# Two decoder layers on one Trainium2 core: the opening's norms and fills re-ordered, and three small loads moved to another queue

## The chip, the cores and the metric

The kernel runs as one program on one core of a Trainium2 chip. Its engines work side by side, each through its own queue in the queue's order: TensorE (PE, with its weight loads shown as PEld), VectorE (DVE), ScalarE (ACT), GpSimd (POOL) and SyncE (SP, which here only issues transfers). ACT and POOL issue transfers too. An engine waits for another by a semaphore, and what stands behind a waiting instruction in the same queue waits with it. The metric is device microseconds (us) of one execution; the figure of a kernel is the median of several.

## The reference

The input is a batch of B = 2 sequences of 1024 tokens with 128 channels, float32 throughout. Two layers follow one another; each adds an attention and then a feed-forward to `x`, each on a layer norm of `x`:

```python
x = x + _L0_attn_ref(_layernorm(x, axis=-1), Wq, bq, Wk, bk, Wv, bv, proj)   # causal, 16 heads of 64
x = x + _L0_ffn_ref(_layernorm(x, axis=-1), W, Wp, bp, sim, temp, Wd0, Wu0, ...) # low-rank experts, top 1 of 4
x = x + _L1_attn_ref(_layernorm(x, axis=-1), W_k, W_v, W_o)                  # 16 heads of 8, scores by distance
x = x + _L1_ffn_ref(_layernorm(x, axis=-1), Wr1, br1, Wr2, br2, Ws1, ...)    # 8 experts, top 2, and a shared one
```

with

```python
def _layernorm(x, axis=-1, eps=1e-05):
    m = jnp.mean(x, axis=axis, keepdims=True)
    v = jnp.var(x, axis=axis, keepdims=True)
    return (x - m) / jnp.sqrt(v + eps)
```

Only the opening of the first layer is touched by the change: the first layer norm, the transposition of its result and of the weights, and some constants.

## The kernel before

The 2048 tokens are 16 tiles of 128 (tokens on the partitions, channels along the row), and lie in `x` as [128, 16, 128]. For loads, norms and the first projections four tiles go together as a group of 512 tokens; groups 0 and 1 are the first sequence, 2 and 3 the second. Four transfers on SP's queue (L80) bring them in this order.

The opening, up to about 41 us, has these steps:

- Loads of the attention's weights `nat_q`, `nat_k`, `nat_v` as [128, 8, 128] (L259): the first of eight chunks of each on ACT's queue, then the biases `bnat`, then the other seven chunks on ACT and SP. After them come the weights of later parts: `proj`, `raw_*` on SP, and `vnat`, `wr`, `br`, `raw_be`, `be` on POOL. The last three on SP's queue are `simI`, `bp` and `temp` (L298, L300, L302), small inputs of the expert choice.
- `layernorm_T(b)` (L117 to L135) for the two groups of a sequence: `bn_stats` and `bn_aggr` for four tiles (L123, L124), then the reciprocal root by `rsqrt`: a bound on VectorE (L99), a logarithm and an exponential on ScalarE (L102, L103), and one refining step of four small VectorE operations (L106 to L109, each 128x4). Then four `tensor_scalar` make the normalized tiles `xn` (L130; three buffers are there for them), TensorE transposes each (L134), and one VectorE copy of 128x512 brings the four from PSUM to `xnT` (L135).
- `turn_nat` transposes chunks of the weights on TensorE, four to a PSUM bank, and VectorE copies them to `wqkvT`: the first chunk of all three together (L327), the other 21 chunks in six copies (L325). The banks of kind `tr`, into which all these transposes go, are four.
- `project(units[0])` makes the queries, keys and values of the first pair of heads of the first sequence, from groups 0 and 1. For q and k a half of the group's product (64 output rows, 512 columns) is one matmul on half of the array; ScalarE takes q (L421) and v (L437) out of PSUM, VectorE k (L429). The banks of kind `acc` are four.
- `small_weights()` transposes and combines the other parts' weights, with a path that goes back and forth between TensorE, VectorE, ScalarE and, for the mask of `bd`, POOL (L388, L392). It reads `simI`, `bp` and `temp`.
- `sides_of_rows()` makes `side_of`, four columns that the second layer's attention uses: a memset of `row` (128x512) and six small ones (L332, L337), a product with the identity (L339), all on POOL, and a sum on VectorE (L340).
- `fill(own[0], G)` presets two column ranges of a buffer of the second layer's attention: 128x2816 and 128x128 elements, strided, on POOL (L171, L172).

In this part a scheduler orders each engine's queue. It decides from its own estimates which ready instruction goes next, so an engine's order is not the order of the source: before, the statistics of all four groups stand ahead of the first refining step on VectorE, and POOL's work for `row` and `own` stands behind its loads.

From the first scores (`scp`, L69) on, the queues of PE, DVE, ACT and POOL are written out by hand (`manual_schedule`), item by item: scores of a tile pair, softmax, transposes (`flipp`, L501), the product with v (`zp`), and in the gaps the projections of the next heads and the feed-forward. It is the larger part of the time; the change leaves its orders as they are.

Of the kernel before, what the change touches and what calls it, by code (L numbers as in the profile page):

```python
# [9 lines left out]
FP = mybir.dt.float32  # L10
AF = mybir.ActivationFunctionType
ALU = mybir.AluOpType
AX = mybir.AxisListType

P = 128
EPS = 1e-5
# [4 lines left out]
def two_layers(ctx: ExitStack, tc: tile.TileContext, a: dict, out: bass.AP):  # L21
    nc = tc.nc
    V, S, G, T = nc.vector, nc.scalar, nc.gpsimd, nc.tensor

    B, SEQ, D = a["L0_attn_x"].shape
# [5 lines left out]
    NG = TOK // 512  # L31
# [3 lines left out]
    NP = a["L0_ffn_Wp"].shape[0]  # L35
    H1, DK = 16, 8
# [7 lines left out]
    small = ctx.enter_context(tc.tile_pool(name="small", bufs=4))  # L44
# [10 lines left out]
    def bank(tag):  # L55
        n, size = banks["tags"][tag]
        return banks["pool"].tile([P, size, 512], FP, tag=tag, name=f"{tag}p", bufs=n)
# [4 lines left out]
    def tr():  # L62
        return bank("tr").rearrange("p o (j q) -> p (o j) q", q=P)
# [7 lines left out]
    def bcast(ap, axis, shape):  # L71
        return ap.unsqueeze(axis).to_broadcast(list(shape))
# [11 lines left out]
    ident = const.tile([P, P], FP, name="ident")  # L84
# [10 lines left out]
    def rsqrt_parts(y, v, least, op):  # L95
        c = small.tile(list(v.shape), FP, tag="rsq", name="rsq")

        def bound():
            V.tensor_scalar(c, v, least, None, op)  # L99

        def guess():
            S.activation(y, c, AF.Ln)  # L102
            S.activation(y, y, AF.Exp, scale=-0.5)  # L103

        def refine():
            V.tensor_tensor(c, c, y, ALU.mult)  # L106
            V.tensor_tensor(c, c, y, ALU.mult)
            V.tensor_scalar(c, c, -0.5, 1.5, ALU.mult, ALU.add)  # L108
            V.tensor_tensor(y, y, c, ALU.mult)  # L109

        return bound, guess, refine

    def rsqrt(*of):
        for part in rsqrt_parts(*of):
            part()


    def layernorm_T(b):
        for g in range(b * NG // B, (b + 1) * NG // B):
            mv = small.tile([P, 4, 2], FP, tag="mv", name="mv")  # L120
            for j in range(4):
                st = small.tile([P, V.BN_STATS_DIM], FP, tag="st", name="st")
                V.bn_stats(st, x[:, 4 * g + j, :])  # L123
                V.bn_aggr(mv[:, j, :], st)  # L124
            rstd = small.tile([P, 4], FP, tag="rstd", name="rstd")
            rsqrt(rstd, mv[:, :, 1], EPS, ALU.add)
            t = tr()
            for j in range(4):
                xn = work.tile([P, D], FP, tag="xn", name="xn")
                V.tensor_scalar(  # L130
                    xn, x[:, 4 * g + j, :], mv[:, j, 0:1], rstd[:, j : j + 1],
                    ALU.subtract, ALU.mult,
                )
                T.transpose(t[:, j, :], xn, ident)  # L134
            V.tensor_copy(xnT[:, bass.ts(g, 512)], t.rearrange("p j q -> p (j q)"))  # L135

    def transposed(dst, src):

        n, m = src.shape
        t = tr()  # L140
        T.transpose(t[:m, 0, :n], src, ident[:n, :n])
        V.tensor_copy(dst, t[:m, 0, :n])
# [19 lines left out]
    side_of = const.tile([P, 4], FP, name="side_of")  # L162
    pre = ExitStack()
    pp0 = pre.enter_context(tc.tile_pool(name="pre", bufs=1, side="right"))
    own = [pp0.tile([P, NB, H1, 32], FP, name="own0")]
# [4 lines left out]
    def fill(side, eng):  # L170
        eng.memset(flat(side, slice(DK + 2, 32)), 0.0)  # L171
        eng.memset(flat(side, slice(DK + 2, DK + 3)), 1.0)  # L172
# [55 lines left out]
    with ExitStack() as l0:  # L228
# [22 lines left out]
        stage = early.enter_context(tc.tile_pool(name="stage", bufs=1))  # L251
# [5 lines left out]
        def load_nat(eng, i, cs):  # L257
            w = a[f"L0_attn_W{'qkv'[i]}"].rearrange("h d e -> (h d) e").rearrange("(c p) e -> p c e", p=P)
            eng.dma_start(nat[i][:, cs, :], w[:, cs, :])  # L259

        for i in range(3):
            load_nat(nc.scalar, i, slice(0, 1))
        bnat = stage.tile([2 * NC, P], FP, name="bnat")
        for i, k in enumerate("qk"):
            nc.scalar.dma_start(
# [4 lines left out]
        load_nat(nc.scalar, 0, slice(1, NC))  # L270
        load_nat(nc.sync, 1, slice(1, NC))
        load_nat(nc.scalar, 2, slice(1, NC))
        vnat = stage.tile([H, 2, DH], FP, name="vnat")
        for r in range(2):
            nc.gpsimd.dma_start(vnat[:, r, :], a["L0_attn_bv"])
# [14 lines left out]
        for i in range(4):  # L290
            r = slice(roff[i], roff[i] + ranks[i])
            nc.sync.dma_start(raw["wd"][r, :], a[f"L0_ffn_Wd{i}"])
            for j in range(2):
                nc.sync.dma_start(
                    raw["wu"][:, j * DH + r.start : j * DH + r.stop], a[f"L0_ffn_Wu{i}"]
                )
        simI = stage.tile([NP, 4 + NP], FP, name="simI")
        nc.sync.dma_start(simI[:, :4], a["L0_ffn_sim"])  # L298
        bp = stage.tile([NP, 1], FP, name="bp")
        nc.sync.dma_start(bp, a["L0_ffn_bp"].unsqueeze(1))  # L300
        temp = stage.tile([P, 1], FP, name="temp")
        nc.sync.dma_start(temp, a["L0_ffn_temp"].partition_broadcast(P))  # L302
        nc.gpsimd.dma_start(wr1, a["L1_ffn_Wr1"])
        nc.gpsimd.dma_start(br1, a["L1_ffn_br1"].unsqueeze(1))
        nc.gpsimd.dma_start(wr2, a["L1_ffn_Wr2"])
# [6 lines left out]
        xnT = xnp.tile([P, TOK], FP, tag="xnT", name="xnT")  # L312
        xn2T = xnp.tile([P, TOK], FP, tag="xnT", name="xn2T")

        def turn_nat(*which):

            t, at = tr(), 0
            for i, cs in which:
                for c in cs:
                    T.transpose(t[:, at, :], nat[i][:, c, :], ident)  # L320
                    at += 1
            i, cs = which[0]
            if len(which) == 1:
                dst = wqkvT[:, i, cs[0] * P : (cs[-1] + 1) * P]
                V.tensor_copy(dst, t[:, :at, :].rearrange("p j q -> p (j q)"))  # L325
            else:
                V.tensor_copy(wqkvT[:, :, cs[0] * P : (cs[0] + 1) * P], t[:, :at, :])  # L327

        def sides_of_rows():

            row = stage.tile([P, 4, 4, 32], FP, name="row")
            G.memset(row, 0.0)  # L332
            for k, part, value in (
                (0, slice(0, DK), 1.0), (0, slice(DK + 1, DK + 2), 1.0), (1, slice(DK, DK + 1), 1.0),
                (2, slice(0, DK), 2.0), (2, slice(DK, DK + 1), 1.0), (3, slice(DK + 1, DK + 2), 1.0),
            ):
                G.memset(row[:, k, :, part], value)  # L337
            row = row.rearrange("p k h j -> p k (h j)")
            G.tensor_tensor(row, row, bcast(ident, 1, [P, 4, P]), ALU.mult)  # L339
            V.tensor_reduce(side_of, row, AX.X, ALU.add)  # L340

        def small_weights():
            sc, dn, pr = D + NR, D, D + NR + 4
# [159 lines left out]
        def keep(it, hh):  # L503
            i = it["i"]
            copy = (V.tensor_copy, S.copy)[hh]
            copy(  # L506
                it["group"]["pT", hh][:, : i + 1, i % 2].rearrange("p j r u -> p r j u"), it["t", hh]
            )
# [238 lines left out]
                    items.append(units[n + 1]["items"][i])  # L747
        items += [units[-1]["items"][i] for i in (2, 3, 0, 1)]
        tail = items.index(units[-2]["items"][4])
        turn_nat(*[(i, [0]) for i in range(3)])  # L750
        transposed(bqk, bnat)

        V.tensor_scalar(bqk[:, :NC], bqk[:, :NC], -SC, None, ALU.mult)
        layernorm_T(0)
        for piece in project(units[0]):
            piece()
        layernorm_T(1)
        for i in range(3):
            for cs in (range(1, 5), range(5, NC)):
                turn_nat((i, cs))  # L760
        transposed(bz, vnat.rearrange("h r d -> h (r d)"))
        V.tensor_scalar(bz, bz, SC, None, ALU.mult)
        small_weights()
        sides_of_rows()
        early.close()
        pp = l0.enter_context(tc.tile_pool(name="pp", bufs=3))
        tp = l0.enter_context(tc.tile_pool(name="tp", bufs=1))
# [5 lines left out]
            mybir.EngineType.PE, mybir.EngineType.DVE, mybir.EngineType.Activation, mybir.EngineType.Pool  # L773
        }
        l0.enter_context(tc.manual_schedule(engines=order))
        fill(own[0], G)
        n = 0
        events = {}
        turns = []
# [595 lines left out]
    with ExitStack() as f1:  # L1375
# [4 lines left out]
        xnT = xnT1[0]  # L1380
# [160 lines left out]
```

## Time and profile before

| what | value |
|---|---|
| median of 3 runs | 1081.24 us (1080.89, 1081.24, 1086.43) |
| profiled execution | 1079.92 us |
| its span, first to last instruction | 1078.2 us |
| granted TensorE clock, mean | 0.978 |
| busy: PE, ACT, DVE, POOL | 94%, 63%, 56%, 32% of the span |
| share of the chain that ended last | PE 80%, DVE 10%, ACT 6% |
| first scores of the first layer's attention | 40.99 us after the start |

A row of the timeline gives the start in us, the duration in us of the run of like instructions that it merges, the engine, the line of the kernel, the operation, what it writes and reads, and in brackets how long the engine had been idle and what ended that. A row of the chain of work that ended last gives the start, the time that the step takes on the chain, and engine, output and line. In the table of stretches the columns are the stretch, its length, the busy time and number of instructions of PE, PEld, DVE, ACT and POOL, the granted clock, the share of the DMA engines and GB/s.

### The profile page before, as it was taken

How to read it: one execution, taken by the hardware profiler on the slowest of the kernel's cores; microseconds unless marked ns; L12 is line 12 of the kernel's file. 1: busy time of each engine (PE TensorE's matmuls, PEld its weight loads, DVE VectorE, ACT ScalarE, POOL GpSimd, SP SyncE). 2: the span in 40 equal slices, each digit the busy share in tenths (PEclk: the TensorE clock that was granted, in tenths of full speed). 3: DMA queues.
4: the chain of work that ended last, by engine and by line, in shares of the span. 5: the costliest groups of instructions: out<-in, count | busy, mean ns of one | idle time of the engine just before them, and what ended most of it. 6: DMA issues, size and time to landing. Idle time of an engine off the chain costs nothing.

```text
span 1078.2 us, 26161 instructions
## 1 busy us (share of the span) xinstructions
PE 1009.4 (94%) x10662; PEld 610.0 (57%) x10662; DVE 599.8 (56%) x1770; ACT 680.9 (63%) x1294; POOL 340.4 (32%) x480
## 2 busy tenths in 40 slices
PE   4899999999999999999788989999999999789998
PEld 1466767666666666666566323323333332679986
DVE  6676676787878878686675323301433310365652
ACT  1376666666666666666465767788776788534541
POOL 4133344343534444434353110000001221023764
PEclk9899999999999999999999999999999999888999
DMA  5000000000000000000001400000000100011222
GB/s 131 1 2 2 2 2 2 2 2 2 2 2 2 2 3 2 1 2 2 2 2 61 117 1 2 2 1 1 20 2 6 30 18 16 10 30 46 79 79 57
DMA packets 27574, 20.13 MB, mean 19 GB/s; under 512 B 3699, under 2 KB 25054, under 8 KB 27454
## 3 DMA queue, kind: packets, MB, share of 16 engines
q1 hardware_dynamic: 22350, 12.17, 4.0%
q0 software_dynamic: 2816, 5.17, 1.9%
q8 instruction: 84, 1.38, 0.6%
q10 hardware_dynamic: 2288, 1.12, 0.4%
q14 instruction: 36, 0.29, 0.1%
HBM read 13.34 MB, written 5.11 MB: 17 GB/s over the span
## 4 chain that ended last, share of the span: by engine, by line
PE 80%; DVE 10%; ACT 6%; issue 2%; DMA 0%; POOL 0%; SPq 0%; DVEq 0%; POOLq 0%; ACTq 0%
PE accp L69 27%; PE bigp L69 14%; PE scp L69 11%; PE zp L69 10%; PE flipp L501 8%; PE upp L69 5%; PE trp L69 3%; ACT pT L506 2%; ACT p L471 1%; DVE pT L506 1%; PE trp L1203 1%; DVE p L467 1%; PE trp L197 1%; ACT e L1175 1%; DVE rsq L108 1%
## 5 line engine op out<-in xcount | busy, mean ns | idle before, releaser
L1175 ACT ACTIVATE e<-bigp 128x1024 f32<-128x1024 f32 x256 | 247.7, 1021 | 80.7 <-PE bigp L69 67.7
L483 POOL TENSOR_SCALAR p<-p,rz 128x384 f32<-128x384 f32 (+7 forms) x256 | 187.6, 745 | 289.9 <-DVE rz L480 264.3
L471 ACT ACTIVATE p<-p,nmax 128x384 f32<-128x384 f32 (+7 forms) x256 | 196.2, 769 | 25.0 <-DVE nmax L467 24.2
L467 DVE CUSTOM_DVE_ANT_0 p<-scp,mask 128x384 f32<-128x384 f32 (+7 forms) x256 | 183.4, 754 | 27.9 <-PE scp L69 16.8
L506 ACT COPY pT<-flipp 128x128 f32<-128x128 f32 (+7 forms) x128 | 81.4, 636 | 146.7 <-PE flipp L501 139.7
L69 PE MATMUL scp<-k,q 64*128 64x512 f32 (+3 forms) x768 | 163.4, 505 | 0.5 <-DVE m L398 0.5
L69 PE MATMUL bigp<-rT,lT 32*128 32x512 f32 x1024 | 158.8, 647 | 0.0
L69 PEld LDWEIGHTS zp<-pT,v 128*64 128x64 f32 x2560 | 136.2, 137 | 26.9 <-issue 8.3
L69 PE MATMUL zp<-pT,v 128*64 128x128 f32 (+1 forms) x2560 | 146.5, 265 | 1.8 <-DVE zT L530 1.1
L501 PEld LDWEIGHTS flipp<-ident,p 64*128 64x128 f32 x2304 | 92.5, 140 | 96.3 <-issue 46.0
L69 PE MATMUL accp<-e,own 128*32 128x512 f32 x1024 | 141.2, 614 | 0.0
L506 DVE COPY pT<-flipp 128x128 f32<-128x128 f32 (+7 forms) x128 | 96.0, 750 | 59.2 <-PE flipp L501 59.0
L501 PE MATMUL flipp<-ident,p 64*128 64x64 f32 x2304 | 111.6, 229 | 16.9 <-DVE rz L480 13.8
L1039 POOL DMA_INDIRECT xs<-rows,from x46 | 46.2, 1003 | 241.4 <-DVE top L1059 156.8
L69 PEld LDWEIGHTS bigp<-rT,lT 32*128 32x128 f32 x1024 | 50.7, 184 | 108.9 <-issue 73.0
L69 PEld LDWEIGHTS scp<-k,q 64*128 64x128 f32 x768 | 69.9, 190 | 38.0 <-issue 30.8
L1302 ACT ACTIVATE hs<-upp,w 128x128 f32<-128x128 f32 x176 | 50.1, 369 | 49.3 <-issue 22.6
L69 PE MATMUL accp<-xnT,wqkvT 128*64 128x512 f32 x256 | 71.1, 622 | 2.0 <-ACT o L608 0.8
L69 PEld LDWEIGHTS accp<-e,own 128*32 128x32 f32 x1024 | 20.9, 108 | 66.2 <-issue 65.5
L421 ACT ACTIVATE q<-accp,bqk 128x512 f32<-128x512 f32 x32 | 37.2, 1162 | 30.2 <-PE accp L69 29.6
L69 PE MATMUL upp<-xsT,w 128*128 128x128 f32 x352 | 49.7, 287 | 4.3 <-DVE xsT L1291 3.9
L1192 DVE COPY cs<-accp 128x512 f32<-128x512 f32 x16 | 11.0, 690 | 73.0 <-PE accp L69 73.0
(325 smaller groups left out, 1149.0 us busy)
## 6 DMA issues: line engine op xcount, KB each, us to landing
given<-y SPq DMA_DIRECT2D x10, 256.0 KB, 2.3
wx<-in_L_ffn_We_dram SPq DMA_DIRECT2D x1, 2048.0 KB
wx<-in_L_ffn_We_dram SPq DMA_DIRECT2D x8, 256.0 KB, 5.4
x<-in_L_attn_x_dram SPq DMA_DIRECT2D x4, 256.0 KB, 4.3
rows<-xn SPq DMA_DIRECT2D x4, 256.0 KB, 2.3
out_dram<-x SPq DMA_DIRECT2D x4, 256.0 KB, 2.3
xs<-rows,from POOLq DMA_INDIRECT x46, 2.5
proj<-in_L_attn_proj_dram SPq DMA_DIRECT2D x1, 512.0 KB
```

Source lines behind the costliest of these rows:

```text
L69: T.matmul(o, lhsT=lhsT, rhs=rhs, start=start, stop=stop)
L108: V.tensor_scalar(c, c, -0.5, 1.5, ALU.mult, ALU.add)
L421: S.activation(q[:, 4 * j : 4 * j + 4].rearrange("p i r u -> p i u r"), t.rearrange("p (i u r) -> p i u r", r=2, u=DH), AF.Identity, bias= ...
L467: V.tensor_tensor_reduce(out=p[:, :n], in0=it["sc"][hh], in1=mask[:, SEQ - n :], scale=1.0, scalar=-NEG, op0=ALU.add, op1=ALU.min, accum_o ...
L471: S.activation(p[:, :n], p[:, :n], AF.Exp, bias=nmax, scale=-1.0, accum_out=it["sum"][:, hh : hh + 1],)
L483: G.tensor_scalar(p[:, :n], p[:, :n], r[:, hh : hh + 1], SC, ALU.mult, ALU.mult)
L501: T.transpose(it["t", hh][:, r, j, :], it["p"][hh][rs, bass.ts(j, P)], ident[rs, rs])
L506: copy(it["group"]["pT", hh][:, : i + 1, i % 2].rearrange("p j r u -> p r j u"), it["t", hh])
L1039: G.indirect_dma_start(out=r["xs"][q][:, j, :], out_offset=None, in_=rows[b][:, :], in_offset=bass.IndirectOffsetOnAxis(ap=r["from"][:, i ...
L1175: S.activation(e[:, 2 * pr : 2 * pr + 2, :], sc[pr], AF.Exp, scale=1.0 / math.sqrt(DK))
L1192: V.tensor_copy(cs, state["c"])
L1302: S.activation(h[:, f, :], t[:, f, :], AF.Silu, bias=w[:, I + NF * D + f : I + NF * D + f + 1])
```

## The change

Six things differ.

1. `fill(own[0])` and the memsets of `row` go from POOL to VectorE, and stand in the source ahead of the later loads; the product of `row` with the identity stays on POOL, its sum on VectorE.
2. `layernorm_T(b)` becomes `norm_T(g)`, which returns three pieces for one group: `stats` (with the bound and ScalarE's guess), `normal` (refining, normalizing, transposing) and `keep` (the copy to `xnT`).
3. For groups 0 and 1 the pieces are called in a fixed order, with the transposition of the weights' first chunks among them, in a block in which the queues of VectorE and ScalarE keep the order of the source.
4. Groups 2 and 3 follow after the first projections, one group after the other, in a block of the same kind.
5. `transposed(bqk, bnat)` and the scaling of `bqk` come after groups 0 and 1.
6. The loads of `simI`, `bp` and `temp` move from the end of SP's queue to POOL's queue, ahead of `vnat`.

```diff
-    def layernorm_T(b):
-        for g in range(b * NG // B, (b + 1) * NG // B):
-            mv = small.tile([P, 4, 2], FP, tag="mv", name="mv")
+    def norm_T(g):
+        mv = small.tile([P, 4, 2], FP, tag="mv", name="mv")
+        rstd = small.tile([P, 4], FP, tag="rstd", name="rstd")
+        bound, guess, refine = rsqrt_parts(rstd, mv[:, :, 1], EPS, ALU.add)
+        t = []
+
+        def stats():
             for j in range(4):
                 st = small.tile([P, V.BN_STATS_DIM], FP, tag="st", name="st")
                 V.bn_stats(st, x[:, 4 * g + j, :])
                 V.bn_aggr(mv[:, j, :], st)
-            rstd = small.tile([P, 4], FP, tag="rstd", name="rstd")
-            rsqrt(rstd, mv[:, :, 1], EPS, ALU.add)
-            t = tr()
+            bound()
+            guess()
+
+        def normal():
+            refine()
+            t.append(tr())
             for j in range(4):
                 xn = work.tile([P, D], FP, tag="xn", name="xn")
...
+                T.transpose(t[0][:, j, :], xn, ident)
+
+        def keep():
+            V.tensor_copy(xnT[:, bass.ts(g, 512)], t[0].rearrange("p j q -> p (j q)"))
+
+        return stats, normal, keep
...
+        fill(own[0], V)
+
+        row = stage.tile([P, 4, 4, 32], FP, name="row")
+        V.memset(row, 0.0)
+        for k, part, value in (
...
+            V.memset(row[:, k, :, part], value)
+        row = row.rearrange("p k h j -> p k (h j)")
+        G.tensor_tensor(row, row, bcast(ident, 1, [P, 4, P]), ALU.mult)
...
+        nc.gpsimd.dma_start(simI[:, :4], a["L0_ffn_sim"])
...
+        nc.gpsimd.dma_start(bp, a["L0_ffn_bp"].unsqueeze(1))
...
+        nc.gpsimd.dma_start(temp, a["L0_ffn_temp"].partition_broadcast(P))
...
-        turn_nat(*[(i, [0]) for i in range(3)])
+
+        with tc.manual_schedule(engines={mybir.EngineType.DVE, mybir.EngineType.Activation}):
+            one, two = norm_T(0), norm_T(1)
+            one[0]()
+            two[0]()
+            one[1]()
+            turn_nat(*[(i, [0]) for i in range(3)])
+            one[2]()
+            two[1]()
+            two[2]()
         transposed(bqk, bnat)
 
         V.tensor_scalar(bqk[:, :NC], bqk[:, :NC], -SC, None, ALU.mult)
-        layernorm_T(0)
         for piece in project(units[0]):
             piece()
-        layernorm_T(1)
+        with tc.manual_schedule(engines={mybir.EngineType.DVE, mybir.EngineType.Activation}):
+            for g in range(NG // B, NG):
+                for piece in norm_T(g):
+                    piece()
...
-        sides_of_rows()
+        V.tensor_reduce(side_of, row, AX.X, ALU.add)
...
-        fill(own[0], G)
```

In the queues of the changed kernel, as they are built, VectorE begins with the memsets of `own` and `row`. Then come the statistics of group 0, of group 1 and, interleaved with group 0's refining, of group 2. The sum of `row` stands before the fourth `xn` of group 0. Two small operations on `simI` and `temp` stand between the copy of group 0's `xnT` and the first `xn` of group 1. The statistics of group 3 stand behind the copy of group 2's `xnT`, and both behind the eviction of the first k. On TensorE the transposes of the 21 other weight chunks stand behind the transposes of all four tiles of group 3. On ScalarE the guess for group 3 stands behind the first two evictions of v.

## The prediction

> **What bounds the kernel now.** I read the page first, by engine in the chain of work that ended last:
>
> ```profile
> PE 80%; DVE 10%; ACT 6%; issue 2%; DMA 0%; POOL 0%; SPq 0%; DVEq 0%; POOLq 0%; ACTq 0%
> ```
>
> TensorE carries four fifths. The change leaves every queue from the first scores (40.99 us) on as it is, so what counts is when these scores start, and at which clock; all behind them shifts with them. I therefore read the chain's opening next (start, time on the chain, engine, output, line):
>
> ```profile
> 10.33 3.59 DVE rsq L108 x3
> 13.92 1.38 DVE rstd L109 x3
> ...
> 18.19 1.97 PE accp L69 x2
> 20.16 0.62 PE trp L134 x2
> 20.78 1.90 PE accp L69 x2
> ...
> 23.30 4.74 PE accp L69 x44
> ...
> 31.10 2.60 DVE wqkvT L325 x5
> ...
> 40.99 0.80 PE scp L69 x4
> 41.79 1.90 PE accp L69 x4
> 43.69 1.00 PE scp L69 x4
> ```
>
> To be seen: two VectorE steps of tiny 128x4 operations take 3.59 and 1.38 us; the two halves of q0 are lone matmul groups of 1.97 and 1.90 with transposes between; the 44 instructions of q1, k and v follow from 23.30 to 28.04; then the weights' copies; then the small weights up to the scores. The timeline (its columns are told above) says why the refining stalls and what VectorE waits for before:
>
> ```profile
> 7.24 0.29 DVE L123 BATCH_NORM_STATS2 st<-x 128x6 f32<-128x128 f32 x1 [0.83 <-DMA x<-in_L_attn_x_dram]
> ...
> 10.25 3.65 DVE L108 TENSOR_SCALAR rsq<-rsq 128x4 f32<-128x4 f32 x3
> 10.43 0.54 POOL L332 MEMSET row<- 128x512 f32 x1
> 10.89 2.46 POOL L171 MEMSET own<- 128x2816 f32 x1
> ...
> 13.94 1.27 POOL L339 TENSOR_TENSOR row<-row,ident 128x512 f32<-128x512 f32 x1
> ```
>
> VectorE stands in L108, whose like elsewhere lasts 0.17 (at 19.20), exactly while POOL works through its memsets, and in L109 during POOL's product. The tokens of group 2 land at 7.24. Third, the stretches, for the clock (column before the last two):
>
> ```profile
> 33.50:34.00 0.50, 0.27 (x3) 0.22 (x2) 0.50 (x5) 0.00 (x0) 0.00 (x0) 1.00 0.00 0
> 34.00:34.50 0.50, 0.50 (x2) 0.23 (x2) 0.38 (x4) 0.00 (x0) 0.00 (x0) 0.56 0.00 0
> ...
> 44.00:44.50 0.50, 0.50 (x4) 0.12 (x2) 0.00 (x0) 0.50 (x1) 0.18 (x1) 0.70 0.00 0
> 44.50:45.00 0.50, 0.20 (x4) 0.07 (x4) 0.33 (x1) 0.38 (x1) 0.00 (x0) 1.00 0.00 0
> ```
>
> The share 0.56 puts the fall to half clock at 34.06, 0.70 the return at 44.30: 10.24 us. The clock reads 1.00 before, but lone 512-column passes lasted 0.99 each until about 23.7 and then 0.43 a pair, so TensorE also began slow. Last, the POOL queue's own loads, with us from issue to landing:
>
> ```profile
> vnat<-in_L_attn_bv_dram POOLq DMA_DIRECT2D x2, 4.0 KB, 4.7
> ...
> be<-in_L_ffn_be_dram POOLq DMA_DIRECT2D x1, 4.0 KB, 6.1
> ```
>
> **The change part by part**, as the time at which each step happens.
>
> *Fills on VectorE.* VectorE is free at 0.89. Its memsets `ones` (128 elements, 0.17) and `brow` (51, 0.10) give 0.91 ns per element: 3456 elements 3.15 us, with fixed parts and the six small memsets (0.35 on POOL) 3.65, so the statistics start at 4.55, not 4.08. Four tiles took 1.08 before; with `ones` and `brow` between, group 0 ends at 5.8 and group 1, with its share of waits, at 7.0. Next stands a statistic of group 2, which waits for 7.24 anyway. That wait is the cover; without it the fills cost one for one. Upper end: at the rate of the sum L340 (0.67 per 512) they last 4.9 and end at 5.8, and all is 1.0 late. Taken: 0, since memset rows are nearer than a sum.
>
> *Refining.* From 7.24 there are four statistics (0.19 each), five aggregates (0.08), a bound, a small copy and four refining steps (0.08 each), with two waits: about 1.65. First `xn` at 8.9, before 15.22: -6.3. POOL's product (1.27) and mask selects (0.64) now follow the fills, 4.6 to 6.5, and miss L108.
>
> *To q0.* Three `xn` 0.77, a bound 0.07, the sum of `row` 0.60 (now inside the path, moved from 27.09, where the chain went over TensorE), the fourth `xn` 0.33, its transpose 0.38, the copies of `wqkvT` and `xnT` about 1.1 together: q0 at 12.15, before 18.19: -6.0.
>
> *To q1.* Before 1.97 + 0.62 + 1.90 + 0.62 = 5.11. Now three `xn` and `bnat` lie between the halves (4 x 0.27, the spacing of two transposes at 22.61 and 22.88), and group 1's fourth transpose comes behind the second half, with its copy on the path (0.38 + 0.07 + 0.69): 1.97 + 1.08 + 1.90 + 1.14 = 6.1. q1 at 18.25, -5.05.
>
> *The three loads.* They leave SP's queue, where they were last and nothing waited behind them, and go on POOL's queue ahead of `vnat`, `wr`, `br`, `raw_be`, `be`, which each move back by three issues of about 0.52 (read at 32 us and later: covered). But VectorE's operations on `simI` and `temp` now stand ahead of group 1's `xn`, which the transposes wait for. `temp` issues at about 7.6; with 4.7 to 6.1 us it lands at 12.3 to 13.7. The first `xn` must be under way by 13.75. So 0, or +0.9 at the 7.0 us that `raw_wp` took as the slowest load; taken +0.2. q1 at 18.45.
>
> [...] Row: POOL's issues beside the bound at 5.66 and 7.71 stayed at 0.50 to 0.57, but these bounds are tiny. [...]
>
> *q1, k, v* keep 4.74: v ends at 23.2, before 28.04: -4.85. Clock: -1.0 if full speed comes before q0's second half, +1.9 if two pairs more run slow (1.9 to 2.0 for a pair, as at 41.79, against 1.18 and 0.86 read here); taken 0, between.
>
> *After v* stands what the norms of group 3 were spared before, when their statistics were long done. On one path now, from v's end: transposes of group 2 (copy starts at +0.42), copy 0.60, four statistics 1.06, bound, logarithm and exponential (0.06 + 0.20 + 0.24 + 0.24), four refining steps in a row (0.19 each, as 18.82, 19.00, 19.20), `xn` three times 0.26 and the fourth 0.33, transpose 0.38: +5.1, copy +5.7. Only behind these transposes TensorE may turn the 21 weight chunks, and VectorE makes six copies (3 x 0.60 + 3 x 0.47 = 3.2). At full clock (0.12 a transpose) the copies bound: end at +8.9. At half clock (0.27) TensorE does: 21 x 0.27 = 5.7 from +5.0, and the last copy, end at +11.3. Before: 5.57. So +3.3 to +5.7; taken +4.5, as the clock before fell 6.0 us after v's end, in the middle of these transposes.
>
> [...]
>
> *To the scores* 7.38 as before, less `temp`'s clamp and exponential (0.06 + 0.12), partly beside the path: -0.1.
>
> *Clock at the scores.* Before, the chain ran 3.3 us at half speed from 40.99 on; the return may now come after the same time or up to 3.4 us later, which costs half of that: 0 to +1.7, taken +0.6, as the row before is at the low end.
>
> Sum: -4.85 + 4.5 - 0.1 + 0.6 = +0.15. The profiled execution's own time is 1079.92 (span 1078.2 and 1.7 around it): 1080.1. It lies 1.3 under the median of 1081.24, so on the median 1081.4.
>
> **Rivals.**
> *The gain comes through.* If TensorE stays at full clock after v and through the small weights, the step after v costs 3.3, the scores' rows (0.80 + 1.90 + 1.00) halve to save 1.85, and an early full clock saves 1.0: -4.85 + 3.3 - 0.1 - 1.85 - 1.0 = -4.5, 1076.7; past -5.4 only if small weights too run faster. For: the clock held 6 us after v before. Against: the gap on TensorE is new.
> *Slower: VectorE stands behind `temp`.* Place: between group 0's copy and group 1's `xn`. Price: one for one from a landing at 13.75. To pass +0.5% it has to land at 19.0, 11.4 us after its issue. For: POOL's loads share the DMA engines with the weights until about 14 us. Against: 6.1 is the longest of that queue. At 19.5, 1086.9.
> *The stall stays.* POOL's product and selects (1.91 together) begin only when VectorE's last small memset is done; if that is 3 us later than I have it, they meet the refining again: +1.9 and the delay of 1.0, 1084.3. For: L108 stood through a whole run of POOL work. Against: POOL has a gap from 3.04 to there.
> *Slow clock in more places.* Half clock for two pairs (+1.9), the chunks (+1.2 over what I took) and the scores (+1.1): 1085.6.
>
> **How the numbers follow.** The forecast (within 2.5 us of 1081.4) gets 0.52. The gain partly through, down to -5.4, 0.17; beyond 0.06. The stall or the slow clock, up to +5.4, 0.17; beyond, by `temp` or several windows, 0.08. 0.5%, about what a measurement of this kernel can tell from no change, is 5.4 us: faster 0.06, same 0.86, slower 0.08. The range 1077.0 to 1086.0 leaves out the two tails and a little of the cases beside them.
>
> **What would show it.** In the changed profile: L108's successor at 0.2 us, first `xn` near 8.9, q0 near 12, v's end near 23; then a gap of 3 us on TensorE, the weights' copies ending near 33, the scores near 41. I am wrong if the scores start before 38 or after 45, if a statistic waits for the fills past 8, or if VectorE idles on a POOL load.

## The result and the profile after

The changed kernel takes 1086.85 us (median of 22 runs, 1083.23 to 1091.63), the kernel before 1082.94 in runs interleaved with it (22 runs, 1080.34 to 1086.43). The ratio is 1.0033 with a 95% interval of 1.0021 to 1.0045: slower by 0.33%, some 3.6 us. Run again in a later session (kernels that ran together on one chip are called a session) it came out as 1.0031 (1.0012 to 1.0050), with the kernel before against itself in the same session at 1.0008 (0.9991 to 1.0024). The loss is below the 0.5% that I had set as the bound of no change, but it is real, and the 1086.85 lies over the end of my range at 1086.0. The profiled execution has its own time of 1086.98 and a span of 1085.3.

The changed kernel's chain of waits by engine still has its four fifths on TensorE:

```profile
PE 80%; DVE 10%; ACT 6%; issue 3%; POOL 0%; DVEq 0%; POOLq 0%; ACTq 0%
```

The same chain in the opening of the changed kernel (start, time on the chain, engine, output, line):

```profile
9.58 0.27 DVE xn L137
...
12.74 1.97 PE accp L69 x2
...
18.54 4.54 PE accp L69 x44
23.08 0.49 PE trp L141 x3
23.59 0.69 DVE xnT L144
24.29 0.21 DVE st L127
...
27.80 1.39 PE trp L141 x4
...
31.30 2.23 DVE wqkvT L347 x4
...
39.87 0.80 PE scp L69 x4
```

To be seen: q0 begins at 12.74 in place of 18.19, q1, k and v end at 23.08 in place of 28.04. Then the norm of group 3, VectorE's but for two steps of 0.21 on ScalarE, stands alone on the chain from 24.29 to 27.80, and the scores start at 39.87, only 1.12 earlier than before. The timeline of the changed kernel (start, us, engine, line, operation, and in brackets the idle time before it and what ended it) shows the pieces:

```profile
1.47 2.40 DVE L182 MEMSET own<- 128x2816 f32 x1 [1.47 <-PEq L1546]
...
4.63 0.29 DVE L127 BATCH_NORM_STATS2 st<-x 128x6 f32<-128x128 f32 x1
...
9.04 0.12 DVE L108 TENSOR_SCALAR rsq<-rsq 128x4 f32<-128x4 f32 x1
...
14.10 0.15 DVE L372 TENSOR_SCALAR temp<-temp 128x1 f32<-128x1 f32 x1 [0.73 <-DMA temp<-in_L_ffn_temp_dram]
...
27.80 1.39 PE L141 MATMUL trp<-ident,xn 128*128 128x128 f32 x4 [4.24 <-DVE xn L137]
...
28.98 1.70 PE L342 MATMUL trp<-ident,nat_q 128*128 128x128 f32 x7
```

The refining step L108 lasts 0.12 where it stood 3.65 before. TensorE has a new gap of 4.24 us behind v. The stretches of the changed kernel show the clock there (column before the last two):

```profile
27.00:27.50 0.50, 0.00 (x0) 0.00 (x0) 0.43 (x3) 0.00 (x0) 0.00 (x0) 0.93 0.00 0
...
30.50:31.00 0.50, 0.50 (x5) 0.50 (x4) 0.50 (x2) 0.00 (x0) 0.00 (x0) 0.66 0.00 0
...
37.50:38.00 0.50, 0.00 (x0) 0.00 (x0) 0.46 (x3) 0.00 (x0) 0.32 (x1) 0.67 0.00 0
44.00:44.50 0.50, 0.50 (x2) 0.11 (x3) 0.50 (x4) 0.27 (x1) 0.00 (x0) 0.50 0.00 0
```

The clock falls at 27.4, just before the first transposes after the gap (27.80), returns at 30.8, falls again at 37.7 and returns at 44.5: the weights' transposes now begin at half clock. In the traces of the kernel before and of the changed kernel the clock reads 1.00 or 0.50 and nothing between, and every stretch between two of its changes lasts a multiple of 3.41 us (here 3.41, 6.83 and 6.83). A step of 3.41 us of this grid is called a window from here on.

So the opening went nearly as forecast, and yet the kernel is slower. The two profiles differ by 7.1 us, and none of it is in the opening; 4.9 of it lie behind 1000 us, in the second layer's experts, on whose queues the change does nothing. The experiments had to tell which part of the change costs, and how far such a pair of single executions can be read at all. In what follows times of landmarks are read from the profiled executions; ratios are to the kernel before, run in the same session.

### The profile page after: what moved, and what is told of

The parts are those of the page before. It is cut to its first block, busy times and chain, and to the rows that moved or that the text cites. A ratio compares the mean times of both kernels' runs of the same rounds, so it can differ in the third digit from the quotient of the medians.

```text
span 1085.3 us, 26165 instructions
## 1 busy us (share of the span) xinstructions
PE 1011.8 (93%) x10662; PEld 613.9 (57%) x10662; DVE 600.3 (55%) x1779; ACT 681.4 (63%) x1294; POOL 341.1 (31%) x474
## 3 DMA queue, kind: packets, MB, share of 16 engines
q10 hardware_dynamic: 2288, 1.12, 0.4%
## 4 chain that ended last, share of the span: by engine, by line
PE 80%; DVE 10%; ACT 6%; issue 3%; POOL 0%; DVEq 0%; POOLq 0%; ACTq 0%
PE accp L69 27%; PE bigp L69 13%; PE scp L69 11%; PE zp L69 10%; PE flipp L510 8%; PE upp L69 4%; PE trp L69 3%; ACT pT L515 2%; DVE pT L515 1%; ACT p L480 1%; PE trp L1222 1%; DVE p L476 1%; PE trp L208 1%; ACT e L1194 1%; DVE rsq L107 1%
## 5 line engine op out<-in xcount | busy, mean ns | idle before, releaser
L69 PE MATMUL accp<-w,hs 128*128 128x128 f32 x352 | 49.0, 285 | 3.3 <-ACT hs L1321 3.3
```

The lines of the kernel that those rows point to most:

```text
L69: T.matmul(o, lhsT=lhsT, rhs=rhs, start=start, stop=stop)
```

## The experiments

### Which of the three parts costs

First the three parts one by one, against the three theories of a late loss: queue slots of the late gathers (A), the place of the program in these windows (B), the fills or norms themselves (C).

The loads back on SP's queue:

```
-        simI = stage.tile(...); nc.gpsimd.dma_start(simI[:, :4], ...)   # and bp, temp, ahead of vnat
+        simI = stage.tile(...); nc.sync.dma_start(simI[:, :4], ...)     # and bp, temp, behind raw_wu
```

> The changed kernel with the loads of simI, bp and temp back at the end of SP's queue; fills and norms stay. In the two profiles the changed kernel starts its scores 1.1 us earlier than the kernel before and loses 8 us between 977 and 1036 us, in the stage of the second layer's sparse experts, where loads that gather tokens go through POOL's queue. Theory A (three more loads on POOL's queue shift which queue slots those gathers and their semaphores fall on, so that loads wait for loads they did not wait for before): the late loss goes, 1.0 to 1.5 us faster than the kernel before (1081.5, ratio 0.999). Theory B (the earlier start changes where the program stands in the clock gate's windows of 3.41 us): the loads are nothing, the start of the scores stays within 0.5 us of 39.9, the time stays 3 to 4 us over the kernel before (ratio 1.003). Theory C (the fills or the norms' instructions themselves): as B, ratio 1.003.

Measured 1.0028 (1.0009 to 1.0048); the scores start at 40.91.

The kernel before with only these loads moved:

```
-        nc.sync.dma_start(simI[:, :4], ...)      # and bp, temp
+        nc.gpsimd.dma_start(simI[:, :4], ...)    # ahead of vnat
```

> The kernel before with only the three loads moved to POOL's queue, ahead of vnat. The opening moves by less than 1 us. Theory A (queue slots of the late gathers): 3 to 5 us slower than the kernel before, ratio 1.003 to 1.005, and the loss lies behind 977 us. Theories B (windows of the clock gate) and C (fills or norms): ratio 1.000, within 0.001.

Measured 0.9991 (0.9976 to 1.0007). Theory A is out: where the loads stand changes neither kernel by more than the intervals can tell. This run also shows the old stall plainly. The three issues push POOL's memsets back by 1.4 us, so they miss the refining (its three L108 last 0.30 together) and hit whatever VectorE does next. The timeline of this kernel:

```profile
11.83 3.49 DVE L753 TENSOR_SCALAR bqk<-bqk 128x8 f32<-128x8 f32 x1
12.26 2.46 POOL L171 MEMSET own<- 128x2816 f32 x1
```

An operation of 8 elements a partition, 0.16 us in the kernel before, lasts 3.49 beside POOL's memset.

The fills back on POOL, norms and loads as changed:

```
-        fill(own[0], V)            # and row's V.memsets
+        fill(own[0], G)            # at its place of before; sides_of_rows() with G.memset
```

> The changed kernel with the fills of own and row back on POOL, at their places of before; norms in groups of four and the three loads as changed. The refining of group 0 meets POOL's memsets again, so the scores start 1 to 4 us later than in the changed kernel (39.9). Theory A (queue slots): the late loss stays and the opening's comes on top, ratio to the kernel before 1.004 to 1.006. Theory B (clock gate's windows): the late loss follows the shift; at a start near 41 it goes, ratio 1.000 to 1.001. Theory C, if it is the fills: 1.000 to 1.002; if it is the norms: 1.004 to 1.006.

Measured 1.0043 (1.0023 to 1.0062); the scores start at 42.70. The fills on VectorE are not the loss: with them back on POOL it is at least as large.

A shift of the changed kernel by one pass:

```
+        mm(zs, ident, xnT[:, :512])      # ahead of the first scores
```

> The changed kernel with one more TensorE pass of 512 columns ahead of the first scores (its result is not used): at half clock about 0.95 us, so that the scores start near 40.9, as in the kernel before. Theory B (clock gate's windows): the program stands against the windows as before, the late loss goes, ratio 1.000 to 1.001. Theories A and C: the loss stays and the pass is added, ratio 1.004 (1087.8 for 1083).

Measured 1.0040 (1.0017 to 1.0063), as by A and C; the pass took 2.04 us, not 0.95, since it is two records of 1.0 each; the scores behind it took 0.80, as those of the kernel before at half clock (at 40.99). In this execution q1, k and v took 6.07 in place of 4.54, and all three sevens of weights' transposes took 1.70 each, as those of `nat_q` at half clock in the changed kernel, so the pass began at 42.92 and the scores at 44.90, not near 40.9. Nothing came back in the median, so theory B finds no support, though this profile doesn't show the place in the windows that it asked for. What remained of the change are the norms.

### The norms, and the gap behind v

The norms left to the scheduler, fills and loads as changed:

```
-        with tc.manual_schedule(...): one, two = norm_T(0), norm_T(1) ...
+        layernorm_T(0)  /  layernorm_T(1)       # as before
```

> Fills on VectorE and the three loads on POOL's queue as in the changed kernel, but the norms as before: their order left to the scheduler, which puts the statistics of group 3 ahead of k's copies and lets the weights' transposes run between those of the tokens. Theory D (the loss of the changed kernel is made by the norms' fixed order: the gap of 4.2 us on TensorE behind v, whose half clock makes the weights' transposes and the scores later in many executions): the gap goes, the scores start 3 to 6 us earlier than in the kernel before (35 to 38), and the time is 2 to 6 us under the kernel before, ratio 0.995 to 0.998. Theory E (the opening isn't it: the late stage of the second layer's experts is slower in the changed kernel for whatever shift): the opening's gain is lost late again, ratio 1.000 to 1.003.

Measured 0.9980 (0.9963 to 0.9998); the scores start at 35.42.

The changed kernel with one move in its order:

```
-            for g in range(NG // B, NG):
-                for piece in norm_T(g): piece()
+            a0, a1 = norm_T(NG // B), norm_T(NG // B + 1)
+            for piece in (a0[0], a0[1], a1[0], a0[2], a1[1], a1[2]): piece()
```

> The changed kernel with one move in the fixed order: the statistics of group 3 stand ahead of group 2's copy of xnT, where VectorE is idle during q1, k and v. That takes four statistics and aggregates (1.6 to 1.7 us in the changed kernel) and the bound, logarithm and exponential (0.5) off the path behind v. Theory D: the scores start 2 to 3 us earlier than in the changed kernel, the time falls by as much or more, ratio to the kernel before 0.999 to 1.001. Theory E: no change against the changed kernel, 1.003.

Measured 1.0001 (0.9985 to 1.0018). The gap behind v fell from 4.24 to 1.83 us. One thing more differs: here the scheduler let the first weights' transposes run between those of group 3 (`nat_q` 0.16 behind the first of them, 1.18 in the changed kernel). Counted from that first transpose, the weights' copies end 4.89 later, 5.71 in the changed kernel. The time went as theory D said, but not the landmark: the scores start at 40.74, since q1, k and v lasted 7.15 in this execution.

The changed kernel and the kernel before, once more:

> The changed kernel once more, for a second profiled execution and more times with their granted clock. Theory D: the start of the scores, 39.9 in the first profile, comes out later here or in the next (up to 44), where other windows of the clock gate fall on the weights' transposes. Theory E: 39.9 within 0.3, and the difference between executions lies behind 900 us. Ratio 1.003 by both.

> The kernel before once more, against itself: ratio 1.000 within 0.002. Theory D: the start of the scores stays at 41.0 within 1 us, the opening depends little on where the windows fall. Theory E: the same, and the stage from 1000 us on ends within 1 us of the first profile, as the first profile's had no gap on TensorE there.

The ratios are given above. The scores start at 40.60 and 40.14: in these two profiles the openings of the two kernels are equal within half a microsecond, and the ratio is 1.0031 all the same.

Then the gap itself. Filled with passes that do nothing, VectorE's chain left as it is:

```
+                if g == NG // B:
+                    idle = bank("acc")[:, 0, :256]
+                    for _ in range(6): mm(idle, ident, xnT[:, g * 512 : g * 512 + 256])
```

> The changed kernel with six TensorE passes of 256 columns (result not used) laid into the gap between the transposes of group 2 and those of group 3: 6 x 0.5 = 3.0 us at full clock, 6.0 at half, in a gap of 3.5 behind group 2's copy. Theory D1 (the gap's cost is the half clock that follows it, on the weights' transposes and the small weights): TensorE stays at full clock through the weights' transposes, the copies (3.2 us) bound them, the scores start near 38 and the time falls by 2 to 3 us, ratio to the kernel before 1.000 to 1.001. Theory D2 (the gap's cost is the serial chain of VectorE's norms itself, not the clock): the scores start no earlier than in the changed kernel (39.9 to 40.9), ratio 1.003; if the clock is half already when the passes begin, up to 2.5 us later, 1.005.

Measured 1.0001 (0.9991 to 1.0011): more work, and no loss is left. That is the time D1 gives, against 1.003 by D2, though the scores start later than its 38. Two things limit this. TensorE's order again has the weights' transposes between those of group 3, as in the kernel with the shorter gap, so the passes are not all that differs. And beside these runs the changed kernel itself ran only once, for a profile, at 1078.51, under the 1079.80 of the kernel before; its 1.0033 and 1.0031 come from runs on other occasions. The shorter gap (1.0001) and the changed kernel (1.0031) were timed together. A second profiled execution of it:

> One more profiled execution of the changed kernel with TensorE kept busy in the gap. In the first, q1, k and v lasted 7.3 us, the scores started at 42.95, and that execution was the slowest of eleven. Theory F: that was a place of the windows that is bad for q1, k and v; where they last 4.5 us, v ends near 23, no half clock falls between the gap and the small weights, and the scores start near 38.

Its timeline on TensorE:

```profile
23.87 2.86 PE L69 MATMUL accp<-xnT,ident 128*128 128x256 f32 x12 [0.78 <-DVE xnT L144]
...
28.59 1.05 PE L342 MATMUL trp<-ident,nat_k 128*128 128x128 f32 x7
...
39.40 0.80 PE L69 MATMUL scp<-k,q 64*128 64x128 f32 x4 [0.47 <-DVE m L407]
```

The passes lie in the gap, and no half clock comes before 33.3 (the clock reads 0.80 from 33.0 to 33.5, then 0.50); the scores start at 39.40 (42.95 in the first, where q1, k and v took 7.31).

Half of the norms undone: the new order for groups 0 and 1, the scheduler's for groups 2 and 3:

```
-        with tc.manual_schedule(...): for g in range(NG // B, NG): ...
+        layernorm_T(1)
```

> The changed kernel with the norms of groups 0 and 1 in the new fixed order and those of groups 2 and 3 left to the scheduler as before. If the step behind v alone makes the loss: v ends near 23, the step behind it is 5.6 as in the kernel before, the scores start at 35 to 36.5, ratio 0.997 to 0.999, as with all norms as before (0.998). If the fixed order of groups 0 and 1 loses too: 1.000 to 1.002.

Measured 0.9969 (0.9956 to 0.9982): the best of all, better than the kernel before and, by the ratios of two sessions, 0.6% better than the changed one. The timeline on TensorE of this kernel:

```profile
23.21 0.55 PE L164 MATMUL trp<-ident,xn 128*128 128x128 f32 x3
...
24.15 0.93 PE L361 MATMUL trp<-ident,nat_q 128*128 128x128 f32 x7
...
36.25 0.80 PE L69 MATMUL scp<-k,q 64*128 64x128 f32 x4 [0.47 <-DVE m L426]
```

v ends at 23.28, as early as in the changed kernel; the weights' transposes follow at once, at 0.13 us each, and their last copy ends 5.80 behind v. The gain of the early q0 comes through. So it is the fixed order of groups 2 and 3 that makes the loss. That it does so by the gap on TensorE is what the kernels with the shorter and the filled gap say, with the limits named there.

### Which clock, and other places

Two more profiled executions, for openings whose windows fall elsewhere:

> One more profiled execution of the changed kernel, for where the clock gate's windows fall in its opening. By theory D the start of the scores lies between 39.9 and 43 according to how many of the windows behind v are at half clock: with the fall near 27 and the return after 10 us 39.9 to 41, with 17 us at half clock 42 to 43.

> One more profiled execution of the kernel before: the start of the scores within 40.0 to 41.2 wherever the windows fall, as the weights' transposes follow v without a gap.

The scores start at 39.97 and 41.10.

> One more profiled execution of the changed kernel, for its opening where the clock gate's windows fall elsewhere. Theory F: with windows at 0.5 to 2.5 us (modulo 3.41) behind the first instruction, q1, k and v last 5.5 to 7.3 and the scores start at 42 or later; with windows elsewhere 4.54 and 39.9 to 41.

Here the windows lay at 1.87, and yet q1, k and v lasted 4.54 and the scores start at 41.24: against theory F as I had drawn its bounds. What was late here is `temp`, in this execution's timeline:

```profile
14.91 0.15 DVE L372 TENSOR_SCALAR temp<-temp 128x1 f32<-128x1 f32 x1 [1.55 <-DMA temp<-in_L_ffn_temp_dram]
```

The transposes behind it began at 15.38 in place of 14.64, and q1 at 19.67 in place of 18.54.

TensorE kept busy from the start, in the changed kernel and in the half-undone one:

```
+        warm = bank("acc")[:, 0, :128]
+        for n in range(10): mm(warm, ident, ident if n < 4 else row[:, n % 4, :])
```

> The changed kernel with ten TensorE passes of 128 columns (result not used) while TensorE has nothing else to do: four from 1.9 us on, six behind the product in row at 6.1, some 5 us at slow speed. In the profiles so far, q1, k and v of the changed opening last 4.54 us in four executions, and 5.6 to 7.3 us in those kernels with its opening whose windows of the clock gate fall 0.5 to 1.5 us behind the first instruction (modulo 3.41). Theory F (the earlier start of q0 comes on a TensorE that has stood since the start, so that by where the windows fall q1, k and v run partly slow): with the passes q0's pair of 0.90 each falls to 0.45, v ends near 21.5 in any execution, the gap behind it stays, and the time falls by 2 to 3 us, ratio to the kernel before 1.000 to 1.001. Theory D1 alone (the half clock behind the gap makes all the loss): v ends up to 1.8 us earlier, the half clock behind the gap stays, ratio 1.001 to 1.003.

> The same ten passes in the kernel that has the new order for groups 0 and 1 alone and the scheduler's for groups 2 and 3 (0.9969 without them). Theory F: q0 is 1.8 us shorter and q1, k and v are fast in any execution, ratio 0.994 to 0.996, the scores start at 34 to 35. If the early slow speed costs nothing beyond what other work covers: 0.997.

Measured 1.0044 (1.0024 to 1.0063) and 0.9988 (0.9971 to 1.0005), neither faster than without the passes. They don't test what they were made for. q0's passes still lasted 1.06 to 1.11 each (0.89 to 1.11 in the changed kernel), and the scheduler put an operation on a POOL load ahead of group 0's fourth `xn`; the timeline of the first:

```profile
12.71 0.15 DVE L365 TENSOR_TENSOR simsq<-simI 32x4 f32<-32x4 f32 x1 [1.05 <-DMA simI<-in_L_ffn_sim_dram]
12.79 0.33 DVE L137 TENSOR_SCALAR xn<-x,mv,rstd 128x128 f32<-128x128 f32 x1
```

q0 started at 15.11 in place of 12.74. Theory F stays untested.

Last, the place of the program in the windows, in the kernel before, with a step of the scores issued twice:

```
-            for o in range(0, n, 512):
+            for o in list(range(0, n, 512)) * (1 + (unit["n"] == 2 and i == 3)):    # the second: i == 5
```

> The kernel before with one scores step of the third unit (512 columns, two heads, at full clock, near 115 us) issued twice: 1.0 us more work on TensorE, which bounds there. In the eighteen profiled executions so far the stretch from about 101 to 790 us, whose queues are the same in all of them, lasts 686.3 to 690.7 us, and its length goes with the place of its start in the clock gate's windows of 3.41 us: 686.7 and 686.3 at 0.05 and 0.57 us behind a window's start, 689.3 at 1.0 to 1.2, 690.7 at 1.34, 688.2 to 688.7 (once 689.1) at 1.5 to 2.2, 689.6 to 689.8 at 2.4 to 2.6. The kernel before stands at 2.4 to 2.6 in three of its four profiles (that with the loads on POOL's queue counted). Theory G (the loss or gain of a shift is made by where the program comes to stand in the windows): 1.0 us later, at 3.4 to 3.6, that is 0.0 to 0.2, the rest of that stretch is about 3 us shorter, so an execution that is 2.0 us faster at 790 us than the kernel before; where it stood at 0.57 it is 3.2 us slower; median of the runs 0.5 to 2.0 us under the kernel before, ratio 0.998 to 0.9995. Theory H (a shift carries through as it is): 1.0 us slower, ratio 1.001.

> The same with the scores step of 768 columns in that unit: 1.4 to 1.5 us more work on TensorE near 120 us. Theory G: from 2.4 to 2.6 it comes to 0.4 to 0.65 behind a window's start, where the stretch lasted 686.3: 3.3 us shorter, 1.8 to 1.9 us faster at 790 us; median 0.5 to 1.9 us under the kernel before, ratio 0.998 to 0.9995. Theory H: ratio 1.0013.

Measured 1.0010 (0.9997 to 1.0023) and 1.0018 (1.0006 to 1.0030). Theory G finds no support: in the median a shift behind the opening carries through as it is. Its premise doesn't hold either, since the kernel before does not stand at one place in the windows; in these two profiles it came to 101 us at 0.36 and 0.99 behind a window's start.

## Why the prediction was wrong

The forecast was 1081.4, and 1086.85 is 5.4 more. Of these 1.7 are the base: the kernel before took 1081.24 in the median of the three runs that I had, and 1082.94 in that of 22. The rest is the change: 3.9 between the medians, where my sum had +0.15.

The steps to the scores held, in part because errors of opposite sign met. *Fills on VectorE*: statistics from 4.63 (4.55 forecast), none waits for the fills past 8. *Refining*: first `xn` at 9.49 instead of 8.9, since each aggregate waited for its statistic (0.40 a tile); the stall in L108 is gone. *To q0* 12.74 (12.15), *to q1* 18.54 (18.45 with the loads).

*The three loads*: `temp` was there at 14.1, later than my 12.3 to 13.7, and VectorE idled 0.73 for it, which I had named as a sign of error. The transposes behind it began at 14.64, with q0's first half running until 14.7, so it cost nothing in this execution. In the fourth, where VectorE idled 1.55, the transposes began 0.7 later. In the median the two runs on the loads show no cost. POOL's issues were not held up much either: the three lasted 0.74, 0.53 and 0.57, the first 0.2 longer than its like before, and the issue that fell beside the three `xn` (at 9.70) 0.57.

*q1, k, v*: 4.54 (4.74). *After v*: from v's end to the last weights' copy 10.43, against 5.65 before: +4.8, and +4.8 to +5.5 in the other profiles (+4.5, at most +5.7). The clock fell 4.35 us behind v's end, and the window of 3.41 us that ended with this fall at 27.43 lay wholly in the gap of 4.24. Not every fall came behind a window that was idle throughout: the one that ended with the fall at 642 us held 1.9 us of waiting (last section). *To the scores* was 0.9 shorter instead of 0.1, because the half clock came at another time (from 37.7, before from 34.06). *Clock at the scores* (+0.6): half clock lasted 4.63 us from the scores on, 3.31 before, and half of the difference is 0.7. The 3.4 that bounds this term is one window: two of the stretches at half clock of the kernel before, from 477.79 and from 822.53 us, last 3.41.

The four profiled executions of the changed kernel start the scores at 39.87, 40.60, 39.97 and 41.24; the kernel before, with the two shifted kernels, which share its opening, at 40.99, 40.14, 41.10, 40.39 and 39.63. The means are 40.42 and 40.45. The kernel with the added pass shares the changed opening and began that pass, in the scores' place, at 42.92; with it the first mean is 40.92. My sum put them at 40.5, so no change at the scores was right within half a microsecond.

The step that failed is the assumption under the sum: "The change leaves every queue from the first scores (40.99 us) on as it is, so what counts is when these scores start, and at which clock; all behind them shifts with them." Queues alike are not times alike. With the scores at nearly the same time the changed kernel is 3.4 us slower than the kernel before (1.0031), and with its gap filled it is not (1.0001), though the scores of that kernel start no earlier (42.95 and 39.40). I priced the gap by the steps that stand in it and the half clock up to the scores and at them; the change costs some 3 us that do not show there.

How it does so stays open; the clock is supported as a part of it. Every timed run gives its mean granted clock. In the session with the changed kernel again it was 0.9776 over 12 runs, against 0.9803 over 35 of the kernel before: 0.0027 x 2 x 1080 = 5.8 us more at half clock. A line through the runs of that session, with a level for each kernel, gives 0.43 us of time per us of half clock, which makes 2.5 of the 3.4. Two things make this an upper end: the kernel before against itself had 0.9794 there, a third of that difference, and the same line in the other sessions has a slope of 0.25 to 0.39. With the gap filled the clock is that of the kernel before (0.9794 and 0.9793), with groups 2 and 3 undone nearly so (0.9788 and 0.9793). Against a simple story: with all norms as before the clock is low too (0.9778), though that kernel is faster.

And the profiles hardly show the place. Half clock from the opening to 1040 us sums to 46.1 us on average in the four of the changed kernel and 44.4 in the five with the opening of before. Four draws from something that varies by 10 us from run to run are too few. One place differs: near 915 us TensorE waits 1.82 us for ScalarE's `h` in either kernel, and behind this wait half clock follows in three of the four profiles of the changed kernel and in none of the five, at a cost of 1.6 us. Whether the timed runs lose time there is not known; the three kernels of the first session with the fixed order don't show it in their one profile each.

Of the rivals, the slow clock in more places (1085.6) came nearest in time and in kind: the weights' transposes ran at half clock, the seven of `nat_q` in 1.70 us against 0.93. But its terms lie ahead of the scores and at them, where no net loss was found, so its nearness in time is luck. The stall did not stay, and VectorE stood behind `temp` at a price in one of the four profiles only (0.7); the two warmed kernels show what that rival costs when `simI` takes its place. *The gain comes through* is what the half-undone kernel does: v at 23.28 and 1075.97 us beside 1079.80 for the kernel before.

## What to carry over

A group moved early is worth what its successors can follow: the early q0 gave TensorE five microseconds, and the fixed order of the next groups handed them back as a gap. Before a norm or any VectorE chain is fixed in order, look for what TensorE has to do meanwhile; leave it work that needs no norm (here the weights' transposes), or the chain and the slow clock behind it are both paid, as here with a gap of 4.24 us and 1.70 us for the seven of `nat_q` in place of 0.93. Take the base of a forecast from as many runs as its result: three were 1.7 us off here. And an equal start of the stage that bounds is not an equal time: where runs spread by half a per cent, take the verdict from interleaved runs and only the mechanism from a profile.

## What was not expected of the hardware

*The last stage has two levels, and they go by the session, not by the kernel.* From about 1000 us to the end the kernels take 78.1 to 78.3 us or 82.0 to 85.2. All four kernels of the first session of experiments took 82.4 to 83.6, all of the second and third 78.1 to 78.3, all of the fourth 82.0 to 85.2, the last two 78.1. The kernel with its gap filled, on one chip, took 78.3 in one session and 82.3 in another. The busy times of 1000 to 1045 us (PE first), changed kernel, first profile:

```profile
1000.00:1045.00 45.00, 41.55 (x363) 40.91 (x362) 22.40 (x58) 24.25 (x88) 29.41 (x28) 1.00 0.25 72
```

The same program, its third profile:

```profile
1000.00:1045.00 45.00, 45.00 (x381) 43.08 (x380) 23.31 (x61) 24.24 (x82) 30.46 (x33) 1.00 0.27 77
```

TensorE is never idle in the second. In the first, the chain of waits has two holes in front of ScalarE's `hs`:

```profile
1019.05 3.25 issue
...
1030.54 3.21 issue
```

What makes them was not found. The two levels account for 4.9 of the 7.1 us between the first two profiles: that of before shows the low one (78.1), that of after the high one (83.0).

*The windows of the clock lie anywhere against the program, and the time of a stretch goes with where it stands in them.* The half-clock stretches in the first profiles of the two kernels last 3.41, 6.83, 10.24, 13.65 or 17.07 us, multiples of one window, and the windows' grid lay anywhere against the first instruction (3.34 us in the kernel before and 0.13 in the changed kernel, in their first profiles; 0.34 in the first of the two executions below, 1.87 in the fourth of the changed kernel, 2.58 in the second with the gap filled). The stretch from about 101 to 790 us, with the same queues and the same instructions, lasted 686.3 to 690.7 in eighteen executions (686.3 where it began 0.57 us behind a window's start, 690.7 at 1.34). Two executions of the kernel before, the stretch of 641 to 650 us (PE first, the clock before the last two columns), first where the clock fell:

```profile
641.00:650.00 9.00, 7.92 (x40) 1.73 (x40) 0.42 (x1) 2.82 (x3) 2.89 (x11) 0.62 0.01 2
```

and where it did not:

```profile
641.00:650.00 9.00, 8.66 (x72) 2.90 (x68) 1.80 (x3) 4.36 (x5) 2.86 (x11) 1.00 0.01 2
```

In front of both TensorE had waited 1.9 us (1.91 and 1.90) for the same product of POOL. In the first the whole wait, 639.91 to 641.82, lay in the window that ended with the fall at 642.05. For the second these rows do not show where its windows lay. In the changed kernel's first profile, where the clock reads 1.00 here too, the windows counted from the fall at 27.43 put a window's end at 641.83, which cuts the same wait (640.36 to 642.26) into 1.5 and 0.4; this is an estimate. So in these executions half clock followed such a wait or did not, and by this estimate it went with how the wait fell. The mean over the places does not reward aiming at one, as the two shifted kernels show (1.0010 and 1.0018).
